# A cross-attention block with its MLP: the same pieces in another written order, score units beside attends

## The chip, the cores and the metric

The kernel runs on one core of a Trainium2 chip. The metric is the device time of one execution in microseconds (us), as a median of several. The core has five engines that run side by side, each through its own instructions in their written order: TensorE (PE, with its weight loads shown apart as PEld), VectorE (DVE), ScalarE (ACT), GpSimd (POOL) and SyncE (SP), which here only issues transfers. They wait for each other through semaphores.

## The reference

Four batches of 512 rows with 512 features, all in float32. Each batch goes through one transformer block with 16 heads of width 32:

```python
x = layer_norm(hidden_states, ln1_w, ln1_b)
q = (x @ q_w + q_b)                          # 16 heads of 32
k = (encoder_hidden_states @ k_w + k_b)
v = (encoder_hidden_states @ v_w + v_b)
scores = einsum("bhqd,bhkd->bhqk", q, k) * scale      # masked
attn = softmax(scores, axis=-1)
out = einsum("bhqk,bhkd->bhqd", attn, v) @ cproj_w + cproj_b
hidden = out + hidden_states
y = layer_norm(hidden, ln2_w, ln2_b)
y = gelu(y @ fc_w + fc_b) @ proj_w + proj_b           # 512 -> 2048 -> 512
return hidden + y
```

## The kernel before

The work is cut into pieces, and a table, `ORDER`, names every step of every piece in the order in which it is written. A loop at the end of the kernel reads the table word by word; each word runs one step of one piece, up to that piece's next `yield`. No scheduler moves anything afterwards: an instruction stands on its engine where its word stands in the table. So the table sets the order on all five engines at once.

The attention is made in 16 windows `w` (batch `w // 4`, a group of four heads `w % 4`). The words that matter here, with the lines of the kernel before:

- `k:w`, `q:w`, `v:w`: the products for K, Q and V of a window on PE (L475, L487, L497), with the copy of the result out of PSUM by ACT. They use the whole 128 x 128 array. A K or Q product is 4 matmuls of 512 columns, a V product 16 of 128 columns. A float32 matmul counts as two instructions in the profile, so these show as x8 and x32.
- `u:w:t`: a score unit (L510), four matmuls, one a head, for 128 query rows `t`. Each uses 32 rows of the array (`32*128` in the profile), the four run at once, and each has its own PSUM bank `sc0` to `sc3`. There is only one set of these four banks.
- `x:w:t`, four words: for each head DVE adds the mask, finds the minimum and moves the scores out of the bank (L518), then ACT takes the exponential (L521).
- `r:w:t`: DVE turns the exponentials in 32 x 32 blocks (L529, L536), two heads at a time; in odd `t` the reciprocal of the row sums (L533) and its own turn (L539) come too.
- `e:w:h` and `d:w:h`: for each half window, twelve transfers of SP and four POOL copies (L546) put the turned blocks where the next product wants them.
- `a:w:h`: an attend, the product of probabilities and V (L568). It uses 32 columns of the array (`128*32`), 16 matmuls, x32 in the profile; DVE then multiplies by the reciprocals (L574).
- `c:b:t`: the output projection (L443); `t1`, `t2` are transposes by PE (L369), `f:b:c` and `P:b:n` the products of the MLP (L621, by a Strassen-like scheme), `fs` the sums of weights that they need (POOL, for most), `j` their joins (ACT copies and DVE additions), `g` the gelu.
- `s1`, `s2`: layer-norm statistics by DVE. `wk`, `wq`, `wv`, `lx`, `lh`, `lf`, `le`: loads that SP issues.

K, Q, V, attends, `c` and the MLP's products take their PSUM result from a ring of four banks.

```python
def scores(w, qt):
    for h in range(HG):
        r = slice(h * HD, (h + 1) * HD)
        nc.tensor.matmul(sc[h], S["qT", w][r, ts(qt, P)], S["kT", w][r, :], start=True, stop=True)
```

Of the kernel before, what the change touches and what calls it, by code (L numbers as in the profile page):

```python
# [77 lines left out]
u:2:3 r:2:1 v:4 x:2:3 x:2:3 k:6 e:1:1 e:1:1 e:1:1 e:2:0 e:2:0 e:2:0 wv:7 d:1:1 na:1 wa:1 na:1 r:2:2 x:2:3 x:2:3 r:2:3
  r:2:3 wa:1 na:1 wa:1 na:1 d:2:0 a:1:1
u:3:0 r:2:2 k:6 wa:1 x:3:0 a:1:1 x:3:0 x:3:0 x:3:0 r:2:3 r:2:3 q:5  # L80
u:3:1 x:3:1 v:5 wv:6 e:2:1 e:2:1 e:2:1 wk:7 wq:7 d:2:0 r:3:0 q:5 x:3:1 x:3:1 x:3:1 v:5 d:2:1 r:3:0 r:3:1 r:3:1 r:3:1
  d:2:1 cb:0 v:3 a:2:0 v:7
u:3:2 q:4 x:3:2 x:3:2 x:3:2 x:3:2 q:4 a:2:0 r:3:1 lf:0:3 e:3:0 e:3:0 e:3:0
u:3:3 a:2:1 q:7 r:3:2 x:3:3 x:3:3 x:3:3 x:3:3
u:4:0 k:7 d:3:0 d:3:0 a:2:1 r:3:2 r:3:3 r:3:3 m:1 r:3:3 r:3:3 x:4:0 x:4:0 x:4:0 x:4:0
u:4:1 r:4:0 v:7 x:4:1 x:4:1 x:4:1 v:6 e:3:1 e:3:1 wv:9 e:3:1 lf:0:2 x:4:1 v:6
u:4:2 r:4:0 r:4:1 a:3:0 x:4:2 x:4:2 k:7 r:4:1 a:3:0 x:4:2 r:4:1 r:4:1 x:4:2 c:0:1 d:3:1 v:4 d:3:1
u:4:3 r:4:2 c:0:0 a:3:1 x:4:3 x:4:3 q:7 x:4:3 c:0:1 r:4:3 x:4:3 c:0:0
u:5:0 r:4:2 r:4:3 x:5:0 x:5:0 a:3:1 x:5:0 x:5:0 c:0:2
u:5:1 c:0:3 s2:0 r:4:3 wk:8 lh:0 d:4:0 cb:0 c:0:2 s2:0 s2:0 r:4:3 le:2 lx:2 le:2 lf:0:1 wq:6 s1:2 wk:9 lh:0 e:4:0  # L90
  e:4:0 e:4:0 le:2 le:2 c:0:0 v:7 fs:0:0 fs:0:0 cb:0 d:4:0 fs:0:1 x:5:1 c:0:3 fs:0:0 m:1 v:6 c:0:1 d:4:1 e:4:1 q:6
  wv:8 e:4:1 e:4:1 d:4:1 x:5:1 r:5:0 x:5:1 x:5:1 a:4:0
u:5:2 v:9 k:8 s2:0 r:5:0 x:5:2 r2:0 r:5:1 n2:0 r:5:1 n2:0 r:5:1 r:5:1 q:6 x:5:2 x:5:2 k:8 x:5:2 c:0:2 c:0:3 n2:0
u:5:3 a:4:0 n2:0 x:5:3 t2:0:1 t2:0:1 r:5:2 t2:0:0 t2:0:0 x:5:3 r:5:2 x:5:3 k:9 a:4:1 x:5:3 r:5:3 v:9 k:9 y:0
u:6:0 x:6:0 d:5:0 fs:0:1 fs:0:1 d:5:0 t2:0:3 t2:0:2 x:6:0 t2:0:2 x:6:0 x:6:0 a:4:1 v:8 f:0:0 t2:0:3 j:0:0 r:5:3 r:5:3
  y:0
u:6:1 y:0 f:0:0 f:0:1 f:0:0 e:5:0 lx:2 wk:10 lx:2 s1:2 lt:2 lt:2 e:5:0 e:5:0 lf:0:3 r:5:3 e:5:1 lx:2 x:6:1 y:0 v:8
  r:6:0 x:6:1 f:0:1 j:0:0 f:0:0 x:6:1 j:0:0 j:0:1 x:6:1 r:6:0
u:6:2 f:0:1 j:0:1 j:0:0 f:0:0 f:0:1 j:0:0 x:6:2 s1:2 r:6:1 r:6:1 j:0:1 f:0:2 fs:0:1 fs:0:2 d:5:1 fs:0:2 s1:2 r1:2
  x:6:2 j:0:1 f:0:1 j:0:1 x:6:2 j:0:0 x:6:2 r:6:1 ts:2 a:5:0 a:5:0 j:0:1 r:6:1  # L100
u:6:3 g:0:0 g:0:0 ts:2 g:0:1 x:6:3 x:6:3 j:0:2 lf:0:4 e:5:1 wk:11 lt:2 lf:0:4 e:5:1 wv:10 wq:8 e:6:0 fs:0:2 d:5:1 k:10
  ts:2 fs:0:2 fs:0:3 lb:2 e:6:0 lb:2 d:6:0 fs:0:3 d:6:0 f:0:2 f:0:2 r:6:2 x:6:3 x:6:3 r:6:2 r:6:3 j:0:2 k:10 r:6:3
  r:6:3
u:7:0 f:0:2 j:0:2 x:7:0 x:7:0 x:7:0 x:7:0 a:5:1
u:7:1 fs:0:4 e:6:0 v:10 wv:11 lf:0:5 a:5:1 r:6:3 e:6:1 lh:1 lf:0:5 x:7:1 v:10 x:7:1 r:7:0 lt:2 fs:0:4 fs:0:3 na:2
  g:0:0 na:2 na:2 fs:0:4 d:6:1 cb:1 a:6:0 x:7:1 x:7:1 wa:2 r:7:0 r:7:1 j:0:2 a:6:0 r:7:1
u:7:2 f:0:4 j:0:4 x:7:2 f:0:4 f:0:4 x:7:2 j:0:4 f:0:2 f:0:4 j:0:2 x:7:2 wa:2 j:0:4 fs:0:4 f:0:3 x:7:2 j:0:4 f:0:4
  r:7:1 e:6:1
u:7:3 na:2 g:0:1 j:0:4 wa:2 wa:2 g:0:4 r:7:1 j:0:4 q:8 q:8 g:0:4 d:6:1 d:7:0 d:7:0 e:6:1 lf:0:6 lf:0:6 fs:0:6 g:0:4
  f:0:3 lh:1 lh:1 e:7:0 e:7:0 e:7:0 x:7:3 x:7:3 r:7:2 x:7:3 x:7:3 a:6:1  # L110
u:8:0 a:6:1 j:0:2 r:7:3 r:7:2 m:2 x:8:0 r:7:3 j:0:3 x:8:0 v:11 x:8:0 x:8:0 r:7:3 a:7:0 wq:9 wq:10 lx:3
u:8:1 f:0:3 r:7:3 a:7:0 j:0:3 v:11 x:8:1 s1:3 e:7:1 fs:0:3 lf:0:7 e:7:1 e:7:1 r:8:0 x:8:1 d:7:1 cb:1 g:0:1 x:8:1 x:8:1
  r:8:1 c:1:1 c:1:1 f:0:3 g:0:2 q:10
# [806 lines left out]
```

## Time and profile before

| | |
|---|---|
| median of 3 runs | 760.53 us (760.25 to 760.59) |
| profiled execution, first to last instruction | 758.0 us |
| DVE busy | 596.2 us (79%) |
| ACT busy | 403.3 us (53%) |
| POOL busy | 371.4 us (49%) |
| DMA, mean share of the 16 DMA engines in use by 40 slices | 0.4 to 0.9 |

The profile names a group of instructions by line, engine and operation, then what it writes and reads (`sc<-pbt` reads `pbt` and writes `sc`), the shape, and how many. In its timeline the first number is the start and the second the duration, in us from the start of the span. Matmuls overlap their neighbours, so the step from one start to the next is the time that a piece costs, and the duration is longer than this step.

### The profile page before, as it was taken

What the parts mean: (1) busy time and instruction counts of PE and PEld (TensorE: products, weight loads), DVE (VectorE), ACT (ScalarE), POOL (GpSimd) and SP (SyncE); (2) the same over time, 40 slices, a digit from 0 to 9 for tenths busy, and PEclk for the clock granted to TensorE, in tenths of its full rate; (3) what the DMA queues carried; (4) which work ended last, traced back from release to release, by engine and by line L of the source; (5) the groups of instructions that cost most, each with busy time, mean ns of one, the idle gap of its engine ahead of it and who ended that gap; (6) DMA issues with size and microseconds to landing.
All of it is one profiled execution on the core that took longest, in us unless ns stands there. A gap on an engine that the chain in (4) does not pass through costs nothing.

```text
span 758.0 us, 14114 instructions
## 1 busy us (share of the span) xinstructions
PE 751.1 (99%) x4925; PEld 534.0 (70%) x4925; DVE 596.2 (79%) x1209; ACT 403.3 (53%) x951; POOL 371.4 (49%) x401
## 2 busy tenths in 40 slices
PE   9999999999999999999999999999999999999998
PEld 6464555467665456665555677766888999999997
DVE  3798999999768888877778986644689799786982
ACT  2566766456777776778867686861343221211110
POOL 1155864743884656656757657854411022240232
PEclk9999999999999999999999999999999999999999
DMA  7698978877887898784977698789545648788575
GB/s 267 199 240 235 251 212 246 232 193 218 212 236 211 229 251 254 204 246 128 248 221 211 209 271 248 219 277 317 163 140 178 247 134 162 225 169 263 99 180 112
DMA packets 72133, 162.18 MB, mean 214 GB/s; under 512 B 11960, under 2 KB 24656, under 8 KB 70400
## 3 DMA queue, kind: packets, MB, share of 16 engines
q1 hardware_dynamic: 56864, 131.44, 59.7%
q0 software_dynamic: 15056, 29.84, 15.9%
q8 instruction: 39, 0.64, 0.4%
q14 instruction: 30, 0.25, 0.1%
q10 hardware_dynamic: 144, 0.02, 0.0%
HBM read 73.95 MB, written 25.18 MB: 131 GB/s over the span
## 4 chain that ended last, share of the span: by engine, by line
PE 96%; DVE 2%; DMA 1%; issue 0%; POOL 0%; ACT 0%; POOLq 0%; DVEq 0%
PE acc L621 37%; PE sc L621 11%; PE sc L510 9%; PE acc L475 8%; PE acc L487 8%; PE acc L443 7%; PE acc L568 7%; PE acc L497 7%; PE acc L369 1%; DMA pbt<-fc_w_dram 1%; PE acc L850 1%; DVE ext L333 0%; DVE swap L330 0%; DVE yT L330 0%; DVE xn L330 0%
## 5 line engine op out<-in xcount | busy, mean ns | idle before, releaser
L521 ACT ACTIVATE ptt<-ptt,mn 128x512 f32<-128x512 f32 x256 | 182.9, 716 | 78.0 <-DVE mn L518 77.5
L518 DVE CUSTOM_DVE_ANT_0 ptt<-sc,mix 128x512 f32<-128x512 f32 x256 | 164.6, 680 | 30.5 <-PE sc L510 29.1
L546 POOL COPY swap<-swap 32x1088 f32<-32x1088 f32 x128 | 139.8, 1092 | 70.0 <-DVE swap L539 43.9
L529 DVE STREAM_TRANSPOSE swap<-ptt 128x1024 f32<-128x1024 f32 x64 | 78.8, 1232 | 9.5 <-DMA pbt<-fc_w_dram 3.2
L536 DVE STREAM_TRANSPOSE swap<-ptt 128x1024 f32<-128x1024 f32 x64 | 78.3, 1224 | 1.8 <-ACT ptt L521 1.8
L510 PE MATMUL sc<-pbt 32*128 32x512 f32 x512 | 73.8, 640 | 0.8 <-ACT pbt L489 0.8
L669 POOL DMA_DIRECT2D gd<-st x32 | 24.4, 766 | 96.9 <-ACT st L667 87.0
L646 ACT COPY st<-acc 128x256 f32<-128x256 f32 x96 | 34.5, 368 | 69.6 <-PE acc L621 66.3
L497 PEld LDWEIGHTS acc<-ptt,ext 128*128 128x128 f32 x512 | 58.7, 192 | 8.7 <-issue 3.4
L621 PE MATMUL acc<-ys,wsum 128*128 128x256 f32 x256 | 64.1, 382 | 0.0
L568 PE MATMUL acc<-swap,mix 128*32 128x256 f32 x1024 | 61.6, 382 | 0.0
L497 PE MATMUL acc<-ptt,ext 128*128 128x128 f32 x512 | 60.8, 277 | 0.0
L646 ACT COPY xn<-acc 128x128 f32<-128x128 f32 x75 | 18.9, 270 | 77.4 <-PE acc L621 72.5
L621 PE MATMUL acc<-yT,pbt 128*128 128x256 f32 x240 | 58.9, 386 | 1.0 <-DVE mix L574 1.0
L475 PE MATMUL acc<-ext,ptt 128*128 128x512 f32 x128 | 59.1, 605 | 0.0
L487 PE MATMUL acc<-ext,ptt 128*128 128x512 f32 x128 | 58.4, 600 | 0.0
L443 PE MATMUL acc<-mix 128*128 128x512 f32 x128 | 58.0, 600 | 0.0
L621 PEld LDWEIGHTS acc<-yT,pbt 128*128 128x128 f32 x240 | 44.0, 190 | 19.7 <-issue 6.9
L621 PEld LDWEIGHTS acc<-ys,wsum 128*128 128x128 f32 x256 | 47.6, 190 | 12.0 <-POOL wsum L330 1.5
L568 PEld LDWEIGHTS acc<-swap,mix 128*32 128x32 f32 x1024 | 30.6, 109 | 31.4 <-issue 9.0
L330 DVE TENSOR_TENSOR st<-acc,st 128x512 f32<-128x512 f32 (+1 forms) x48 | 26.1, 544 | 32.0 <-ACT st L646 22.4
L521 ACT ACTIVATION_READ_ACCUMULATOR ptt<-ptt,mn 128x1 f32 x256 | 48.3, 189 | 0.0
(143 smaller groups left out, 1396.7 us busy)
## 6 DMA issues: line engine op xcount, KB each, us to landing
swap<-swap SPq DMA_DIRECT2D x384, 136.0 KB, 3.4
gd<-st POOLq DMA_DIRECT2D x32, 512.0 KB, 4.7
swap<-gd SPq DMA_DIRECT2D x12, 1024.0 KB, 5.8
pbt<-fc_w_dram SPq DMA_DIRECT2D x40, 256.0 KB, 4.3
xn<-x_dram SPq DMA_DIRECT2D x32, 256.0 KB, 5.3
ext<-fc_w_dram SPq DMA_DIRECT2D x24, 256.0 KB, 2.9
swap<-xn POOLq DMA_DIRECT2D x18, 256.0 KB, 4.7
ptt<-k_w_dram SPq DMA_DIRECT2D x16, 256.0 KB, 4.0
```

The source lines that it names most:

```text
L443: nc.tensor.matmul(acc, oT[:, g, ts(t, P)], wc[:, g, :], start=(g == 0), stop=(g == NG - 1))
L475: nc.tensor.matmul(acc, S["wk", w][:, d, :], eT[:, d, :], start=(d == 0), stop=(d == ND - 1))
L487: nc.tensor.matmul(acc, S["wq", w][:, d, :], xT[:, d, :], start=(d == 0), stop=(d == ND - 1))
L497: nc.tensor.matmul(acc[:, ts(t, P)], eT[:, d, ts(t, P)], S["wv", w][:, d, :], start=(d == 0), stop=(d == ND - 1),)
L510: nc.tensor.matmul(sc[h], S["qT", w][r, ts(qt, P)], S["kT", w][r, :], start=True, stop=True)
L518: nc.vector.tensor_tensor_reduce(out=s, in0=sc[h], in1=mb, scale=1.0, scalar=FMAX, op0=ALU.add, op1=ALU.min, accum_out=mn)
L521: nc.scalar.activation(s, s, AF.Exp, bias=mn, scale=-1.0, accum_out=S["sums", w][:, qt, h : h + 1])
L529: nc.vector.transpose(*two_heads[0])
L536: nc.vector.transpose(*two_heads[1])
L546: nc.gpsimd.tensor_copy(pT[ts(i, HD), i], tb[ts(i, HD), i])
L568: nc.tensor.matmul(av[ts(h, HD), : 2 * P].rearrange(shape, **kw), v[:, t, ts(h, HD)], p[t][h], start=(t == 0), stop=(t == NT - 1),)
L621: nc.tensor.matmul(o, x[:, k], y[:, k], start=(k == 0 and not more), stop=(k == n - 1), skip_group_check=more)
```

## The change

Only the table `ORDER` is written anew. It holds the same words, each as often as before; the functions, tiles and instructions are the same. Because the table is five lines shorter, every line after it has a number smaller by 5 (L510 becomes L505). Two lines of each side:

```diff
-u:2:1 r:1:3 x:2:1 e:1:0 lb:1 e:1:0 lb:1 lt:1 lt:1 lf:0:1 wq:5 wk:6 wv:4 cb:0 d:1:0 v:2 d:1:0 d:1:1 x:2:1 q:3 r:2:0 v:5
...
-u:2:2 r:2:0 x:2:2 x:2:2 x:2:2 x:2:2 r:2:1 r:2:1 a:1:0 v:4
+u:2:1 e:1:1 a:1:0 e:1:1 e:1:1 v:5 x:2:1 x:2:1 k:5 x:2:1 x:2:1
+u:2:2 x:2:2 x:2:2 r:2:1 x:2:2 lt:1 lt:1 x:2:2 v:4 wv:7 na:1 r:2:1 v:4 r:2:1
```

A few counts over the PE order of both programs. Steps between a piece on the whole array and a piece in tiles (score unit or attend), either way: 138 before, 114 now. Score unit and attend next to each other: 25 before, 34 now. Score unit, one attend, score unit, with nothing between: none before, 7 now; two more have only the 8-column transpose of `ts` (L392) beside the attend. Two attends in a row: 2 before, 5 now. On ACT, loads of a function table: 40 before, 34 now.

The first place is on PE, at the second score unit of window 2. Before, a V product and an attend stand between this unit and the next:

```order
L510 MATMUL sc_74<-pbt 128x512
L510 MATMUL sc_75<-pbt 128x512
L510 MATMUL sc_76<-pbt 128x512
L510 MATMUL sc_77<-pbt 128x512
L497 MATMUL acc_79<-ptt,ext 128x128 x16
L568 MATMUL acc_78<-swap,mix 32x256 x16
```

Now the attend alone stands there:

```order
L505 MATMUL sc_74<-pbt 128x512
L505 MATMUL sc_75<-pbt 128x512
L505 MATMUL sc_76<-pbt 128x512
L505 MATMUL sc_77<-pbt 128x512
L563 MATMUL acc_80<-swap,mix 32x256 x16
```

In both the next row writes `sc_74` again. What moved away is the V product, which follows the second unit now.

The second place is on DVE, after the last of the four mask-and-minimum steps of unit 3 of window 0 (`mn_0_3_3`). Before, the turns of the finished unit are spread among the steps of the next one and two statistics:

```order
L536 STREAM_TRANSPOSE swap_104<-ptt_107 128x2x4x4x32
L529 STREAM_TRANSPOSE swap_104<-ptt_107 128x2x4x4x32
L533 RECIPROCAL rsum_0_1_386<-sums_0_220 128x8
L518 ISA ptt_107,mn_1_0_0_398<-sc0_74,mix_103 128x512
L518 ISA mn_1_0_0_398 128x1
L341 BN_STATS st1_1_0_402<-xn4_86 128x6
L342 BN_AGGR mv1_1_401<-st1_1_0_402 128x2
L536 STREAM_TRANSPOSE swap_104<-ptt_107 128x2x4x4x32
L539 STREAM_TRANSPOSE swap_104<-mix_103 128x2x4x32
```

Now all turns stand in one block ahead of the steps of unit 0 of window 1:

```order
L524 STREAM_TRANSPOSE swap_104<-ptt_107 128x2x4x4x32
L531 STREAM_TRANSPOSE swap_104<-ptt_107 128x2x4x4x32
L528 RECIPROCAL rsum_0_1_405<-sums_0_233 128x8
L531 STREAM_TRANSPOSE swap_104<-ptt_107 128x2x4x4x32
L534 STREAM_TRANSPOSE swap_104<-mix_103 128x2x4x32
L513 ISA ptt_107,mn_1_0_0_416<-sc0_74,mix_103 128x512
L513 ISA mn_1_0_0_416 128x1
L513 ISA ptt_107,mn_1_0_1_419<-sc1_75,mix_103 128x512
L513 ISA mn_1_0_1_419 128x1
```

The statistics went to other places. On PE, a K and a V product stood between the units 0 and 1 of window 1; now a K product alone.

The third place is SP, right after the Q weight of window 1 (`wq:1`). Before, the weight of V for window 1 comes next and the Q weight of window 2 is the fourth of these rows:

```order
L327 DMA ptt_107<-v_w_dram 128x512
L327 DMA xn4_86<-x_dram 128x512
L327 DMA pbt_106<-fc_w_dram 128x512 x2
L327 DMA ptt_107<-q_w_dram 128x512
L327 DMA ptt_107<-v_w_dram 128x512
L327 DMA ptt_107<-k_w_dram 128x512 x2
```

Now the load for the residual (`xn4`) and two of the next batch's rows (`xn5`, `xn0`) stand ahead, and the Q weight of window 2 is the tenth of these rows:

```order
L322 DMA xn4_86<-x_dram 128x512
L322 DMA pbt_106<-fc_w_dram 128x512
L322 DMA xn5_87<-x_dram 128x512
L322 DMA ptt_107<-v_w_dram 128x512
L322 DMA xn0_82<-x_dram 128x512
L322 DMA ptt_107<-v_w_dram 128x512
L322 DMA pbt_106<-fc_w_dram 128x512
L322 DMA ptt_107<-k_w_dram 128x512
L322 DMA pbt_106<-fc_w_dram 128x512
L322 DMA ptt_107<-q_w_dram 128x512
```

More of the change, by code (lines that the diff above doesn't have):

```diff
@@ L78 @@
[L78 to L113, printed above, removed]
@@ new lines @@
+u:8:0 m:2 r:7:2 x:8:0 r:7:3 f:0:3 e:7:0 e:7:0 j:0:3 x:8:0 v:11 x:8:0 r:7:3 r:7:3 x:8:0 a:6:1
+u:8:1 x:8:1 x:8:1 f:0:3 j:0:3 wq:10 d:7:0 r:8:0 fs:0:3 q:10 x:8:1 x:8:1 e:7:1 wq:9 j:0:3 f:0:3 j:0:3 d:7:1 g:0:2 g:0:2
+  e:7:1 q:10
+u:8:2 a:7:0 r:8:0 j:0:3 g:0:3 x:8:2 fs:0:5 x:8:2 fs:0:5 r:8:1 x:8:2 r:8:1 f:0:5 r:8:1 e:7:1 a:7:0 c:1:1 c:1:1 d:7:1
+  r:8:2 r:8:1 v:11 q:9 x:8:2
+u:8:3 x:8:3 q:9 x:8:3 wk:11 e:8:0 x:8:3 x:8:3 a:7:1 j:0:5 a:7:1
+u:9:0 r:8:3 k:11 r:8:3 r:8:3 e:8:0 e:8:0 fs:0:5 lx:3 le:3 r:8:3 r:8:2 wq:11 d:8:0 x:9:0 x:9:0 lx:3 d:8:0 le:3 le:3
+  cb:1 x:9:0 x:9:0 r:9:0 r:9:0 c:1:2 f:0:5 f:0:5 c:1:2
```

269 lines of the change are left out of this document (146 added, 123 removed).

## The prediction

> **What bounds the kernel now.** I read the page first, then the busy time by stretches, then PE's waits, then PE's timeline.
>
> ```profile
> span 758.0 us, 14114 instructions
> PE 751.1 (99%) x4925; PEld 534.0 (70%) x4925; DVE 596.2 (79%) x1209; ACT 403.3 (53%) x951; POOL 371.4 (49%) x401
> 20.00:200.00 180.00, 179.18 (x1143) 97.99 (x1146) 165.12 (x366) 116.46 (x290) 100.07 (x102) 1.00 0.82 224
> 200.00:540.00 340.00, 338.86 (x2034) 216.56 (x2027) 249.46 (x533) 236.60 (x506) 222.79 (x250) 1.00 0.80 232
> PE acc L621 <- DVE mix L574: 1.0, 1, 1.0
> PE sc L510 <- ACT pbt L489: 0.8, 1, 0.8
> ```
>
> PE is the bound: 751.1 of 758.0 us, at the full granted clock (1.00). So the order can help in two ways only, by a cheaper sequence of the same products or by fewer waits of PE, and it can hurt by new waits. The stretch 20 to 200 us names the engine that would cause them: DVE is busy 165.12 of 180 us there (92%; the columns of such a row are PE, PEld, DVE, ACT and POOL, each with its count of instructions, then clock, share of the DMA engines and GB/s).
>
> A busy PE may hide waits inside a piece, so I read steps from start to start.
>
> ```profile
> 33.53 3.70 PE L487 MATMUL acc<-ext,ptt 128*128 128x512 f32 x8
> 37.16 1.14 PE L510 MATMUL sc<-pbt 32*128 32x512 f32 x8
> 38.23 3.84 PE L497 MATMUL acc<-ptt,ext 128*128 128x128 f32 x32
> 42.00 1.14 PE L510 MATMUL sc<-pbt 32*128 32x512 f32 x8
> ...
> 77.85 1.93 PE L568 MATMUL acc<-swap,mix 128*32 128x256 f32 x32
> 79.71 1.14 PE L510 MATMUL sc<-pbt 32*128 32x512 f32 x8
> 80.78 3.84 PE L497 MATMUL acc<-ptt,ext 128*128 128x128 f32 x32
> ...
> 432.77 3.60 PE L487 MATMUL acc<-ext,ptt 128*128 128x512 f32 x8
> 436.20 1.03 PE L621 MATMUL acc<-yT,pbt 128*128 128x256 f32 x4
> ...
> 492.06 3.59 PE acc L568 x64
> ```
>
> A Q product between two score units takes 37.16 - 33.53 = 3.63 us, one between two full-array products 436.20 - 432.77 = 3.43. The 0.20 us is what it costs to go from the full array into tiles and back. A score unit takes 1.07 (38.23 - 37.16; 80.78 - 79.71 right behind an attend), an attend 1.86, a V product between units 3.77.
>
> **The change part by part.** (1) *Fewer changes of the array's mode.* The PE order has 138 steps between a full-array piece and a tiled one, and 114 after the change. 24 fewer are 12 returns, at 0.20 us: -2.4 us. PE sets the end, so this counts in full. Three more pairs of attends in a row gain between nothing and 0.14 us each (one pair in this trace takes 3.59 us, against 2 x 1.86); I leave them in the bounds, -2.8 to -2.0.
>
> The Trainium skill, TensorEngine Tiling (Array Packing), section Key Properties, says that changing the tiling mode drains TensorE, not only leaving tiling. By that, a score unit (row tiles) beside an attend (column tiles) would still drain and this term would be nothing. The trace speaks against it: the unit takes 1.07 us behind a K, Q or V product and behind an attend alike.
>
> (2) *Score units too close for their banks.* There is one set of four score banks, so a unit waits until DVE has read the unit before it. How long that takes:
>
> ```profile
> 33.84 0.40 DVE L539 STREAM_TRANSPOSE swap<-mix 128x256 f32<-128x256 f32 x1
> 34.17 0.65 DVE L518 CUSTOM_DVE_ANT_0 ptt<-sc,mix 128x512 f32<-128x512 f32 x1
> ...
> 38.31 0.69 DVE L518 CUSTOM_DVE_ANT_0 ptt<-sc,mix 128x512 f32<-128x512 f32 x1 [0.49 <-PE sc L510]
> ...
> 38.93 0.69 DVE L518 CUSTOM_DVE_ANT_0 ptt<-sc,mix 128x512 f32<-128x512 f32 x1
> ...
> 40.15 0.69 DVE L518 CUSTOM_DVE_ANT_0 ptt<-sc,mix 128x512 f32<-128x512 f32 x1
> ...
> 40.77 1.24 DVE L536 STREAM_TRANSPOSE swap<-ptt 128x1024 f32<-128x1024 f32 x1
> 41.93 1.20 DVE L529 STREAM_TRANSPOSE swap<-ptt 128x1024 f32<-128x1024 f32 x1
> 43.06 0.16 DVE L533 RECIPROCAL rsum<-sums 128x8 f32<-128x8 f32 x1
> ```
>
> The unit starts at 37.16, DVE reads its first bank from 38.31 (1.15 later), one bank each 0.61 us, and the last is read at 40.15 + 0.69 = 40.84, 3.68 us after the unit began. A turn takes a step of 1.16 us, the reciprocal 0.10 (to the next start at 43.16), its own turn 0.33. That a unit really waits on its last bank, PE being in order, shows where this trace has it once:
>
> ```profile
> 197.36 1.14 PE L510 MATMUL sc<-pbt 32*128 32x512 f32 x8
> ...
> 201.36 1.14 PE L510 MATMUL sc<-pbt 32*128 32x512 f32 x8
> ...
> 206.27 1.93 PE L568 MATMUL acc<-swap,mix 128*32 128x256 f32 x32
> 208.13 1.93 PE L510 MATMUL sc<-pbt 32*128 32x512 f32 x8
> 209.99 1.13 PE L621 MATMUL acc<-yT,pbt 128*128 128x256 f32 x4
> ...
> 206.15 1.25 DVE L529 STREAM_TRANSPOSE swap<-ptt 128x1024 f32<-128x1024 f32 x1 [2.22 <-DMA pbt<-fc_w_dram]
> ...
> 208.19 0.69 DVE L518 CUSTOM_DVE_ANT_0 ptt<-sc,mix 128x512 f32<-128x512 f32 x1
> ```
>
> DVE ends the previous unit's last bank at 208.19 + 0.69 = 208.88, and the unit of 208.13 takes 1.86 us (209.99 - 208.13) in place of 1.07: 0.79 us lost, though the row counts as busy.
>
> Now the new order. In the seven places "unit, attend, unit" the second unit would start 1.07 + 1.86 = 2.94 us after the first; its last bank is free 3.68 + 0.06 after it (0.06 from the end of DVE's step to the head's start): 0.76 us lost. In two places a transpose lies beside the attend and 0.4 us are lost. Behind one pair (window 5) and another (window 12) DVE also has a leftover of 0.25 together. Sum: 7 x 0.76 + 2 x 0.41 + 0.25 = 6.4 us. Before, the nearest two units stand 4.0 us apart (197.36 and 201.36).
>
> Elsewhere it is a run of units that outpaces DVE. Wait = DVE's work since it last waited for a unit + 1.22 (1.15 + 0.06 and rounding) - PE's distance. First case, from unit 3 of window 0 to unit 1 of window 1, the second place of the order: PE has a V and a K product between, 1.07 + 3.77 + 1.07 + 3.63 = 9.54 us; DVE has 8 banks x 0.61 + 3 turns x 1.16 + 0.10 + 0.34 for the row sums = 8.80. Wait: 8.80 + 1.22 - 9.54 = 0.5. The same sum gives 0.7 more up to unit 0 of window 2 (seven units stand 4.7 to 5.0 us apart there, and each unit brings DVE 2.44 + 2.32 us of banks and turns before anything else), 1.0 in windows 2 and 3, 1.1 in windows 4 and 5: 3.3 in all. For the order before, the same sum finds no wait. Together 6.4 + 3.3 = +9.7 us. Bounds: +6.4, where the turns go beside other work; +14.2, where I put durations (1.24, 0.69) in place of steps. I take 9.7, since the steps are what DVE showed back to back. A PE that waits here gives the time back nowhere: all its products stand behind, in order.
>
> (3) *What was lost before.* The wait at 208 (0.79) and the idle 1.0 for DVE's mix right behind it come of one late load (2.22 on `pbt` above); the order there is new, so I take them as gone, -1.8; bounds 0 and -2.8 (all that PE lacks between 20 and 540 us, 0.82 + 1.14, and that 0.79).
>
> (4) *Weight sums nearer to their products.* POOL makes the sums that an MLP product reads.
>
> ```profile
> L333 POOL TENSOR_TENSOR wsum<-pbt,wsum 128x256 f32<-128x256 f32 x20 | 14.8, 746 | 3.0 <-PE acc L621 2.4
> L546 POOL COPY swap<-swap 32x1088 f32<-32x1088 f32 x128 | 139.8, 1092 | 70.0 <-DVE swap L539 43.9 <-DVE mix L574 13.4 <-PE sc L510 8.0
> swap<-swap SPq DMA_DIRECT2D x384, 136.0 KB, 3.4
> ptt<-q_w_dram SPq DMA_DIRECT2D x16, 256.0 KB, 4.2
> 22.17 0.33 SPq L327 DMA_DIRECT2D ptt<-q_w_dram  x1
> 28.69 3.50 PE L497 MATMUL acc<-ptt,ext 128*128 128x128 f32 x29
> L667 ACT ACT_TABLE_LOAD x20 | 25.7, 1283 | 0.3
> ```
>
> Of 32 MLP pieces, 10 have a third sum with less than 1.8 us of PE work between its word and its product; 4 before. Each of the six more can cost a sum of 0.75 us: between 0 and +4.5; I take +1.0, near the low end, because PE's delays of (2) give POOL time.
>
> (5) *At no cost.* The first loads: window 2's Q weight stands behind five more loads, but it waits for its buffer until the first Q product ends (22.17) in both orders. Its product now stands in the place of the V product of 28.69, so 4.2 us to landing leave about 2; without that cover it costs as much as the load is late, 1 to 2 us. Transfers and copies between turn and attend: twelve transfers, issued over 7 us, and 3.4 to landing, beside 4 x 1.09 on POOL, so 10.5 us; the nearest attend in the new order stands 12.5 us behind its turn. Six loads of function tables fewer take 6 x 1.28 us from ACT, which is 53% busy and ends no large wait of PE.
>
> **Sum.** 758.0 - 2.4 + 9.7 - 1.8 + 1.0 = 764.5 us for the profiled execution. The median is 760.53 - 758.0 = 2.5 us longer than that span, so 767.0 us.
>
> **The rivals.** *No change.* Only the pairs wait (+6.4), all old waits go (-2.8), the modes give -2.8: +0.8, 761.3 us. For it: DVE is idle 15 us between 20 and 200, so its turns may fit. Against it: that idle time stands elsewhere than the runs of units.
>
> *Faster.* DVE starts on a unit as soon as its first head is done. In a pair the second unit's heads start apart, as at 208; if DVE's first bank came 0.8 us earlier than 1.15 behind the start, pair waits vanish and the rest shrinks to nothing: 758.0 - 2.4 - 1.8 + 1.0 + 2.5 = 757.3. It decides where 1.15 becomes 0.4. Against it: unit after unit in this trace shows 1.15 or more.
>
> *POOL is late.* All six sums of (4): 767.0 + 3.5 = 770.5. For it: POOL issues transfers too and waits in order; against it: POOL is 49% busy.
>
> *The change doesn't save what it says.* An attend beside a unit drains as well, by a mechanism that the rows above do not show: 767.0 + 2.4 = 769.4 us. That is the quoted rule of the Trainium skill's tiling page.
>
> **How the numbers follow.** 0.66 for the forecast (its own range 763 to 771: 6.4 to 9.7 and some for the waits, 0 to 2.8 for the old ones), 0.12 for no change, 0.08 for faster, 0.10 for late sums, 0.04 for no saving. A measurement of this kernel tells 0.2% (1.5 us) from no change. Faster: 0.08. The no-change rival lies within, with a part of it above: 0.10. Slower: 0.82. The range reaches from the no-change case to the late sums with part of the upper bound of (2): 760.0 to 773.0 us; it leaves out the faster case and the far ends, some 0.15.
>
> **What would show it.** In the profile after: a second unit in each of the seven pairs with a step of about 1.83 us in place of 1.07; a first long unit at window 1, unit 1; Q products next to full-array ones at 3.43 more often; PE's wait list still short, since waits hide inside units. Wrong would be units at 1.07 everywhere (then DVE keeps pace), or PE idle for transfers, POOL sums or first loads, which I hold for small.

## The result, and the profile after

The changed kernel takes 773.85 us (median of 4 runs, 773.17 to 775.47) against 760.39 us (4 runs, 759.61 to 760.59) before. The ratio is 1.0183, 95% interval 1.0168 to 1.0197: slower by 13.5 us. The prediction said 767.0 us and a range of 760 to 773: the side is right, the size is not.

The page of the changed kernel:

```profile
span 771.1 us, 14133 instructions
PE 760.0 (99%) x4925; PEld 543.5 (70%) x4925; DVE 608.8 (79%) x1209; ACT 397.8 (52%) x945; POOL 374.6 (49%) x401
L505 PE MATMUL sc<-pbt 32*128 32x512 f32 x512 | 85.2, 640 | 1.1 <-ACT pbt L484 1.1
```

The score units' row before:

```profile
L510 PE MATMUL sc<-pbt 32*128 32x512 f32 x512 | 73.8, 640 | 0.8 <-ACT pbt L489 0.8
```

The changed kernel's busy time by stretches, in the columns of the prediction's rows:

```profile
20.00:200.00 180.00, 179.22 (x1110) 99.53 (x1109) 161.44 (x356) 111.73 (x279) 100.64 (x101) 1.00 0.81 224
200.00:540.00 340.00, 338.82 (x2025) 216.22 (x2024) 261.57 (x539) 231.84 (x509) 218.42 (x241) 1.00 0.79 228
540.00:771.00 231.00, 223.45 (x1707) 214.53 (x1705) 178.04 (x297) 49.58 (x154) 53.61 (x52) 0.99 0.64 168
```

And PE's longest waits (engine and line, what it waited for, us in total, times, longest):

```profile
PE acc L364 <- DVE xn L357: 2.2, 1, 2.2
PE acc L616 <- ACT xn L641: 2.0, 1, 2.0
PE acc L845 <- POOL nhalf L834: 1.3, 1, 1.3
PE sc L505 <- ACT pbt L484: 1.1, 2, 0.8
```

Line numbers are 5 lower than before. PE is again busy to 99%, and it is "busy" 8.9 us longer with the same 4925 matmuls: the score units alone (L505) rose from 73.8 to 85.2 us. From 20 to 540 us PE idles as long as before, 1.96 us (0.78 + 1.18); behind 540 us it lacks 7.6 us (231.00 - 223.45), where before it lacked 3.6. The row of before:

```profile
540.00:758.00 218.00, 214.41 (x1673) 206.16 (x1671) 174.56 (x295) 46.15 (x151) 45.74 (x42) 1.00 0.66 174
```

Since waits hide in busy time, I took each PE piece's step from start to start and subtracted what it takes where nothing waits: 1.07 us a unit, 1.86 an attend, 0.112, 0.216 and 0.429 a matmul of 128, 256 and 512 columns, and 0.20 a return between the full array and tiles. What is left over, in us:

| | before | changed | difference |
|---|---|---|---|
| ahead of the first unit | 3.80 | 2.84 | -0.96 |
| score units | 0.78 | 12.55 | +11.77 |
| other pieces up to the last attend | 2.20 | 1.51 | -0.69 |
| everything behind the last attend | 1.29 | 7.05 | +5.76 |
| changes of mode | 13.59 | 11.23 | -2.36 |
| the steps themselves (attends in a row are shorter) | | | -0.41 |

The sum is +13.1 us, the difference of the two spans (771.1 - 758.0). The row of the mode changes is their number at a fixed price, a count and not a measurement of its own. The price is the same in both traces: a stretch on the full array between two tiled pieces takes 0.197 us more than its bare steps before and 0.194 now (medians of 68 and 56 stretches).

So there are two losses: the units, and a stretch behind the last attend for which the prediction has no term.

The units first, in PE's timeline of the changed kernel (start, us, engine, line):

```profile
76.65 1.14 PE L505 MATMUL sc<-pbt 32*128 32x512 f32 x8
77.72 1.93 PE L563 MATMUL acc<-swap,mix 128*32 128x256 f32 x32
79.59 1.93 PE L505 MATMUL sc<-pbt 32*128 32x512 f32 x8
81.45 0.82 PE L492 MATMUL acc<-ptt,ext 128*128 128x128 f32 x5
...
114.58 1.24 DVE L524 STREAM_TRANSPOSE swap<-ptt 128x1024 f32<-128x1024 f32 x1
115.30 1.14 PE L505 MATMUL sc<-pbt 32*128 32x512 f32 x8
117.39 0.84 DVE L452 TENSOR_SCALAR mix<-m 128x512 f32<-128x512 uint8 x1
118.38 0.69 DVE L513 CUSTOM_DVE_ANT_0 ptt<-sc,mix 128x512 f32<-128x512 f32 x1
120.00 2.42 PE L505 MATMUL sc<-pbt 32*128 32x512 f32 x8
122.35 0.82 PE L492 MATMUL acc<-ptt,ext 128*128 128x128 f32 x5
```

u:2:2, behind u:2:1 and one attend, steps 1.86 us (81.45 - 79.59): 0.79 lost, as at 208 us before. The unit of 120.00 stands a whole K product behind the last one and still steps 2.35 us: DVE read the first bank of the unit of 115.30 (u:4:0) only at 118.38, 3.1 us behind its start, since turns and a mask tile came first.

Then the stretch behind 540 us:

```profile
543.63 1.82 DVE L357 TENSOR_SCALAR xn<-xn,mv,rs 128x512 f32<-128x512 f32 x2 [1.21 <-POOL rs L352]
545.38 1.21 DVE L328 TENSOR_TENSOR mix<-pbt 128x512 f32<-128x512 f32 x1
546.51 2.22 DVE L325 TENSOR_TENSOR ext<-swap 128x512 f32<-128x512 f32 x1
547.31 0.38 PE L364 MATMUL acc<-ident,xn 128*128 128x128 f32 x2
548.65 1.59 DVE L357 TENSOR_SCALAR xn<-xn,mv,rs 128x512 f32<-128x512 f32 x2
549.85 0.89 PE L364 MATMUL acc<-ident,xn 128*128 128x128 f32 x3 [2.15 <-DVE xn L357]
```

DVE normalises two row tiles of the last batch, then makes two sums (words pt:7 and xs:0:4) that PE does not need yet, then the other two row tiles. PE's next piece is the turn of these tiles, and it waits 2.15 us. Before, the turns stand in one piece:

```profile
539.97 1.91 PE L369 MATMUL acc<-ident,xn 128*128 128x128 f32 x16
```

Right behind this wait the granted clock falls (the third number from the end of a row):

```profile
552.00:554.00 2.00, 2.00 (x9) 1.73 (x8) 2.00 (x4) 0.78 (x2) 0.00 (x0) 0.50 0.00 0
```

It is 0.50 for 3.4 us, from 550.8 us on. PE works there at half speed, which no list of waits shows; by an estimate from these two figures it loses 1.7 us. Of the 5.76 us, 4.0 are then more idle time (7.55 - 3.59) and 1.7 the slower clock.

### The profile page after: what moved, and what is told of

It is laid out like the page before. It is cut to its first block, busy times and chain, and to the rows that moved or that the text cites. A ratio compares the mean times of both kernels' runs of the same rounds, so it can differ in the third digit from the quotient of the medians.

```text
span 771.1 us, 14133 instructions
## 1 busy us (share of the span) xinstructions
PE 760.0 (99%) x4925; PEld 543.5 (70%) x4925; DVE 608.8 (79%) x1209; ACT 397.8 (52%) x945; POOL 374.6 (49%) x401
## 4 chain that ended last, share of the span: by engine, by line
PE 92%; DVE 2%; DMA 2%; POOL 1%; ACT 1%; issue 1%; DVEq 0%; POOLq 0%; ACTq 0%
PE acc L616 35%; PE sc L616 10%; PE sc L505 10%; PE acc L492 8%; PE acc L438 7%; PE acc L563 7%; PE acc L470 7%; PE acc L482 6%; DMA swap<-xn 2%; PE acc L364 1%; PE acc L845 0%; DMA xn<-x_dram 0%; DVE ptt L513 0%; DVE ext L325 0%; POOL ext L328 0%
## 5 line engine op out<-in xcount | busy, mean ns | idle before, releaser
L541 POOL COPY swap<-swap 32x1088 f32<-32x1088 f32 x128 | 141.4, 1104 | 65.0 <-DVE swap L531 24.2
L505 PE MATMUL sc<-pbt 32*128 32x512 f32 x512 | 85.2, 640 | 1.1 <-ACT pbt L484 1.1
L664 POOL DMA_DIRECT2D gd<-st x32 | 23.9, 749 | 85.2 <-ACT st L641 32.5
L563 PEld LDWEIGHTS acc<-swap,mix 128*32 128x32 f32 x1024 | 30.5, 109 | 35.3 <-issue 10.3
L505 PEld LDWEIGHTS sc<-pbt 32*128 32x128 f32 x512 | 27.2, 182 | 32.9 <-DVE mn L513 13.0
```

The source lines that it names most:

```text
L541: nc.gpsimd.tensor_copy(pT[ts(i, HD), i], tb[ts(i, HD), i])
L563: nc.tensor.matmul(av[ts(h, HD), : 2 * P].rearrange(shape, **kw), v[:, t, ts(h, HD)], p[t][h], start=(t == 0), stop=(t == NT - 1),)
```

## The experiments

In a_n2_late, b_pairs and b_doubles some products or sums read an operand before its new contents are written, so their numbers differ; the instructions are the same. Spans are of one profiled execution, ratios are to the kernel before.

### The stretch behind the last attend

**a_tail_b and b_tail_a** exchange the last words (behind u:15:3) between the two orders.

> The changed order up to and with u:15:3, then all remaining words in the order of before. Theory (the changed kernel's 5.9 us of PE waits after 540 us come from how the last words are ordered): 5 to 6 us less than the changed kernel, about 768 us, ratio to before about 1.0105, and PE's waits on DVE's xn (L357) and ACT's xn (L641) gone. Rival (they are inherited from the attention stage, where DVE and POOL fell behind): no gain, 773 to 774 us, ratio about 1.018.

> The order of before up to and with u:15:3, then all remaining words in the order of the change. Theory (the order of the last words alone costs 5.9 us): 5 to 6 us more than before, about 766 us, ratio about 1.0075. Rival (the late stretch is only slow because of what came ahead of it): 760 to 761 us, ratio 1.000.

a_tail_b: 770.42 us, 1.0138 (1.0122 to 1.0153). b_tail_a: 765.43 us, 1.0071 (1.0045 to 1.0096). With before's last words the excess behind the last attend is 1.29 us, with the changed ones 7.04 behind the order of before: it goes with the words alone. The slower clock is not needed for it: in b_tail_a's profiled execution the clock is 1.00 from 525 to 550 us and 1.000 in the mean of the span. Behind the last attend PE is idle 0.9 us longer there than in the changed kernel, and from that attend to the end both take 239.7 us. PE's waits in b_tail_a show the two of the changed kernel:

```profile
PE acc L616 <- ACT xn L641: 2.4, 1, 2.4
PE acc L364 <- DVE xn L357: 2.2, 1, 2.2
```

a_tail_b gained 3.4 us and not 5 to 6, because where the two orders meet (an attend at 502 us) PE waits for something new:

```profile
PE acc L563 <- ACT st L646: 2.6, 1, 2.6
```

**a_n2_first** moves the two sums of the timeline above.

```diff
-n2:3 n2:3 pt:7 xs:0:4 n2:3 n2:3 t2:3:1 fs:3:0 pt:4 ps:6 fs:3:1 pt:3 t2:3:0 t2:3:0
+n2:3 n2:3 n2:3 n2:3 t2:3:1 fs:3:0 pt:4 ps:6 fs:3:1 pt:3 pt:7 xs:0:4 t2:3:0 t2:3:0
```

> The changed order with two words moved: pt:7 and xs:0:4, written between the second and the third step of the last batch's normalisation n2:3, now stand behind its fourth step and ahead of the second turn t2:3:0. Theory (DVE does 3.4 us of sums ahead of the rows that PE must turn): the 2.2 us wait of PE on DVE's xn at 549.9 us goes, 2.2 to 4.3 us less than the changed kernel, 770 to 771.5 us, ratio 1.013 to 1.0155. Rival (the wait was for something else that is late, or the sums are then late for the next product): within 0.5 us of the changed kernel, ratio 1.018.

774.93 us, 1.0196 (1.0172 to 1.0220): no gain. The wait on the normalisation is gone (the turns at 548.43 take 2.06 us in one piece), and another stands right behind:

```profile
548.43 2.06 PE L364 MATMUL acc<-ident,xn 128*128 128x128 f32 x16
```

Among PE's waits of the same kernel:

```profile
PE acc L616 <- DVE yT L372: 2.5, 1, 2.5
```

The turned tiles are evicted by DVE too (yT, L372), and the sums now stand ahead of that.

**a_n2_late and a_n2_late2** were to move all five sums behind the chain.

> The changed order with five words moved: the first pt:7, xs:0:4, pt:4, ps:6 and pt:3 behind the last batch's n2:3, sums on DVE of 0.7 to 1.2 us an instruction, now stand one by one among the joins behind y:3, not ahead of or between the normalisation, the turns and the y sums. Theory (in this stretch the chain norm, turn, y sums, first product runs over DVE, and every sum written into it is paid by PE): the excess of the turns, 3.6 us, and of the products behind them, 0.8 us, goes: 3.5 to 4.4 us less than the changed kernel, about 769.8 us, ratio about 1.013, and the wait on ACT's xn (L641, 2.0 us at 660 us) stays. Rival (DVE has more work up to there than time, in any order): PE waits as long at a later product, ratio 1.017 to 1.020.

> The changed order with five words moved: pt:7 and xs:0:4, written between the second and the third step of the last batch's normalisation n2:3, and pt:4, ps:6 and pt:3, written between its steps and the turns, now stand one by one among the joins behind the y sums y:3. Theory (in this stretch the chain norm, turn, y sums, first product runs over DVE, and every sum written into it is paid by PE; moved only behind the norm, they were paid at the turn's eviction): the turns' excess of 3.6 us and the 0.8 us behind them go, 3.5 to 4.4 us less than the changed kernel, about 769.8 us, ratio about 1.013. Rival (DVE has more to do up to there than there is time for, in any order): PE waits as long at a later product, ratio 1.017 to 1.020.

In a_n2_late the words moved are the next ones of the same names, and the two between the steps of the normalisation stand where they were: the 2.2 us wait stayed, 775.36 us, 1.0201 (1.0186 to 1.0216). a_n2_late2 moves the first ones:

```diff
-n2:3 n2:3 pt:7 xs:0:4 n2:3 n2:3 t2:3:1 fs:3:0 pt:4 ps:6 fs:3:1 pt:3 t2:3:0 t2:3:0
+n2:3 n2:3 n2:3 n2:3 t2:3:1 fs:3:0 fs:3:1 t2:3:0 t2:3:0
...
+y:3 y:3 y:3 pt:5 j:3:0 f:3:1 j:3:1 pt:7 f:3:1 f:3:1
```

771.11 us, 1.0142 (1.0128 to 1.0156), some 3 us less than the changed kernel. The turns' excess falls from 3.58 to 0.26 us. But the products behind 608 us lose 1.95 us more (4.49 in place of 2.54). The second wait is only 0.3 us longer (2.3 in place of 2.0); the rest is the clock, which now falls to 0.50 behind this wait, again for 3.4 us:

```profile
PE acc L616 <- ACT xn L641: 2.3, 1, 2.3
658.00:660.00 2.00, 2.00 (x11) 2.00 (x11) 0.00 (x0) 0.99 (x3) 0.46 (x1) 0.50 1.14 261
```

**a_tail_fix** tried that one.

```diff
-P:1:1 pj:1:1 la:1:7 pj:0:7 pt:7 P:0:7 pj:0:7 P:0:3 pt:1 P:1:1 gs:1:5 P:1:1 P:1:4 gs:1:6 pj:1:1 J:0:4 J:0:6 pj:0:5 J:0:5
+la:1:7 pj:0:7 pt:7 P:0:7 pj:0:7 P:0:3 pt:1 gs:1:5 gs:1:6 J:0:4 J:0:6 pj:0:5 J:0:5 P:1:1 pj:1:1 P:1:1 P:1:1 P:1:4 pj:1:1
```

> The changed order with the five sums behind the y sums (as a_n2_late2) and, besides, the words of batch 1's first two projections that stood ahead of J:0:4, J:0:6 and J:0:5 (P:1:1 three times, pj:1:1 twice, P:1:4) moved behind J:0:5, where the order of before has them. Theory (ACT's copy into xn waits for a row that a transfer still reads, because the next batch's projection is begun before the joins of this one): the wait of 2.3 us on ACT's xn at 657 us goes, and most of the 4.5 us of excess in the products behind 608 us: 2 to 4 us less than a_n2_late2, 767 to 769 us, ratio 1.009 to 1.0115. Rival (the wait is for another row or transfer): 771 us, ratio 1.014.

770.79 us, 1.0144 (1.0129 to 1.0159): the wait is still there (2.6 us), so the rival holds. So it is not these words that take the row too early. In the changed kernel's timeline ACT stands 6.5 us for a transfer that reads xn; which word makes that transfer late stays open.

```profile
660.18 0.27 ACT L641 COPY xn<-acc 128x128 f32<-128x128 f32 x1 [6.51 <-DMA swap<-xn]
```

### Whether the early lateness makes the later one

**b_then_a6** takes before's words up to u:6:0 and the change's from there.

> The order of before up to u:6:0, then all remaining words in the order of the change (124 changes of tile mode). Theory (each stretch's waits belong to its own order): of the changed kernel's excess over before this keeps the score units' waits behind 172 us, 6.5 us, and the 5.9 us behind 540 us, and saves 7 returns, 1.4 us, and 0.5 us of older waits: 10 to 10.5 us more than before, about 770.5 us, ratio 1.0135. Rival (the lateness of DVE in windows 0 to 5 is carried on and makes the later waits): the later score waits shrink to what before has, 0.8 us, and the ratio is 1.006 or less.

776.86 us, 1.0219 (1.0205 to 1.0233). The units' excess is 6.76 us, as forecast, though windows 0 to 5 ran like before, and the stretch behind the last attend is 7.50. So each stretch's waits come from its own words; the rival falls. The total is 6 us above the forecast. At the place where the orders meet PE waits 3.4 us, and the clock is 0.50 for 6.8 us, which by an estimate is up to 3.4 us more:

```profile
PE acc L616 <- DVE st L325: 4.5, 3, 3.4
```

### What a pair of units costs

**a_no_pairs and a_no_pairs2** break eight of the nine pairs by a full-array product between. The second of the eight:

```diff
-u:6:2 x:6:2 x:6:2 a:5:0 ts:2 ts:2 x:6:2 x:6:2 u:6:3 j:0:1 r:6:1 x:6:3 x:6:3 k:10
+u:6:2 x:6:2 x:6:2 a:5:0 ts:2 ts:2 x:6:2 x:6:2 k:10 u:6:3 j:0:1 r:6:1 x:6:3 x:6:3
```

> The changed order with eight of its nine 'unit, attend, unit' pairs broken up: for each, the next full-array product that was written behind the second unit is written ahead of it (c:0:3, k:10, f:0:4 with its two sums, k:11, t2:1:0, f:1:1, f:1:3, c:2:3); the pair of u:2:1 and u:2:2 stays. It has 128 changes of tile mode in place of 114, 7 returns more. Theory (the second unit waits for DVE to leave the score banks): the eight waits in the changed kernel's trace add up to 5.7 us and go; the mode changes cost 7 x 0.20 = 1.4 us; so 4.3 us less than the changed kernel, about 769.5 us, ratio to before about 1.0125. Rival (DVE is simply behind there, and PE will wait for it at the next unit whatever stands between): the waits come back within one or two units and the time is 774 to 775 us, ratio 1.018 to 1.020.

> The changed order with the same eight pairs broken up again, now only by products that have nothing to wait for: c:0:3, k:10, k:11, k:13 and k:14 go ahead of the second unit, and v:10, f:1:4 and c:2:2, written ahead of the first unit, go behind the attend. 128 changes of tile mode, 7 returns more than the changed kernel. Theory (the second unit of a pair waits for DVE to leave the banks, and only there): the eight waits of 5.7 us go, 7 x 0.20 = 1.4 us of mode changes come, 4.3 us less than the changed kernel, about 769.5 us, ratio to before about 1.0125. Rival (DVE or the ring of accumulators is behind there anyway): new waits stand at other pieces of the same windows and the ratio is 1.017 or more.

Both are slower than the change: 778.76 us, 1.0241 (1.0224 to 1.0258), and 780.82 us, 1.0275 (1.0250 to 1.0300). The units' excess falls from 12.55 to 7.77 and 8.60 us, by 4.8 and 4.0 of the 5.7 that were forecast, and the seven returns count for 1.38. But the other pieces' excess rises from 1.51 to 8.36 and 11.36 (by an estimate 1.4 and 1.7 of it come of a clock of 0.50 from 205.7 and 205.6 us on). The largest new wait of both:

```profile
PE acc L616 <- ACT st L641: 3.3, 1, 3.3
```

k:10 stood between u:6:3 and the products f:0:2, and covered ACT's copies out of the accumulators that f:0:2 needs. Moved ahead of the unit, it uncovers them. Both times are above what either forecast of a_no_pairs gives; the rival of a_no_pairs2 (new waits at other pieces) is right. This product was not only a gap between two units, it also covered something.

**b_pairs_min** goes the other way: six pairs in the order of before, by six products moved and nothing else, q:7 for instance. **b_pairs** had tried nine, with the loads and sums beside them moved too: 789.82 us, 1.0392 (1.0375 to 1.0410), with new waits of up to 4.6 us for POOL's sums; it tells little of the pairs.

```diff
-u:3:3 a:2:1 q:7 r:3:2 x:3:3 x:3:3 x:3:3 x:3:3 u:4:0 k:7
+u:3:3 a:2:1 r:3:2 x:3:3 x:3:3 x:3:3 x:3:3 u:4:0 q:7 k:7
```

> The order of before with nine 'unit, full-array product, attend, unit' (or attend first) made into 'unit, attend, unit' and the product behind: at u:2:1, u:2:3, u:3:1, u:3:3, u:4:3, u:7:0, u:7:1, u:8:0 and u:9:3. 120 changes of tile mode in place of 138. Nothing else of the change. Theory: nine second units wait 0.79 us each, 7.1 us, and nine returns less save 1.8 us: 5.3 us more than before, about 765.5 us, ratio 1.007; in the trace the second units step in 1.86 us in place of 1.07. Rival (a pair costs nothing by itself, the units of the changed kernel wait since DVE was behind there for other reasons): 1.8 us less than before, ratio 0.9976.

> The order of before with six full-array products alone moved, so that six 'unit, attend, unit' pairs arise: v:5 behind u:2:2, k:6 behind u:3:0, q:7 behind u:4:0, c:0:0 behind u:5:0, v:11 behind u:8:1, q:11 behind u:9:3. 126 changes of tile mode in place of 138; every other word where it was. Theory: six second units wait 0.79 us each, 4.7 us, six returns less save 1.2 us: 3.5 us more than before, about 763.7 us, ratio 1.0046. First rival (DVE is nearly full in windows 2 to 6, and a unit that is pulled ahead of a 3.5 us product is late by most of that): 1.2 to 2.5 us a pair in the first four, ratio 1.007 to 1.012. Second rival (a pair costs nothing by itself): ratio 0.9984.

b_pairs_min: 775.48 us, 1.0221 (1.0183 to 1.0258), above both forecasts: the first rival's direction, at a higher price. Six returns less count for 1.18 us. The second units lose 10.3 us: 2.76 (u:2:2), 2.18 (u:3:0), 0.79 (u:4:0), 2.53 (u:5:0), 0.44 (u:8:1), 1.61 (u:9:3). Besides, two attends that now come earlier wait 3.5 us for their operands. The longer of these waits (2.9 us) stands between u:8:0 and u:8:1, so DVE had time to read the banks; the 0.44 us of u:8:1 is the clock, 0.57 in the mean from 242 to 246 us. A dear pair and the cheap one, in the timeline:

```profile
74.98 0.69 DVE L513 CUSTOM_DVE_ANT_0 ptt<-sc,mix 128x512 f32<-128x512 f32 x1
75.60 1.24 DVE L524 STREAM_TRANSPOSE swap<-ptt 128x1024 f32<-128x1024 f32 x1
76.73 2.15 PE L505 MATMUL sc<-pbt 32*128 32x512 f32 x6
77.01 0.69 DVE L513 CUSTOM_DVE_ANT_0 ptt<-sc,mix 128x512 f32<-128x512 f32 x1 [0.17 <-DVE swap L524]
77.63 1.24 DVE L524 STREAM_TRANSPOSE swap<-ptt 128x1024 f32<-128x1024 f32 x1
78.79 0.65 DVE L513 CUSTOM_DVE_ANT_0 ptt<-sc,mix 128x512 f32<-128x512 f32 x1
80.56 1.61 PE L492 MATMUL acc<-ptt,ext 128*128 128x128 f32 x12
...
112.56 1.14 PE L505 MATMUL sc<-pbt 32*128 32x512 f32 x8
112.59 1.20 DVE L524 STREAM_TRANSPOSE swap<-ptt 128x1024 f32<-128x1024 f32 x1
113.72 0.69 DVE L513 CUSTOM_DVE_ANT_0 ptt<-sc,mix 128x512 f32<-128x512 f32 x1
115.50 1.93 PE L505 MATMUL sc<-pbt 32*128 32x512 f32 x8
```

Around 75 us two turns stand between the reads of u:2:1's banks, and u:2:2 behind it takes 3.83 us (80.56 - 76.73) in place of 1.07. At 112.59 a turn runs while PE still writes u:3:3; then the banks are read back to back, and u:4:0 loses 0.79. So the distance on PE is one part of the price, and DVE's words between are the other.

**b_pairs_x** keeps the six pairs and moves those words: x words ahead, turns behind.

```diff
-u:3:3 a:2:1 r:3:2 x:3:3 x:3:3 x:3:3 x:3:3 u:4:0
+u:3:3 x:3:3 x:3:3 a:2:1 r:3:2 x:3:3 x:3:3 u:4:0
```

> The order of before with the six pairs of b_pairs_min, and in these six units alone the x words (DVE reads the score banks) moved ahead of the turns and other words, as far as the six score tiles let them: one or two turns of 1.24 us go from ahead of the last x word to behind it at u:2:1, u:4:3, u:8:0 and u:9:2; at u:2:3 the tiles allow no change of weight. Theory (a pair waits for the DVE words between, not for the distance alone): 1.2 us less at three of them, 2.5 us less at u:8:0, about 6 us less than b_pairs_min, 769.5 us, ratio to before about 1.0125. Rival (what is put behind is missed at once, as with all x words moved): 775 us or more, ratio 1.02 or above.

779.65 us, 1.0251 (1.0224 to 1.0278): the rival, no gain over b_pairs_min. u:2:2 gained 0.7 us, but the cheap pair became dear (2.32 us lost in place of 0.79):

```profile
114.05 0.69 DVE L513 CUSTOM_DVE_ANT_0 ptt<-sc,mix 128x512 f32<-128x512 f32 x1 [1.16 <-PE sc L505]
...
115.28 1.24 DVE L524 STREAM_TRANSPOSE swap<-ptt 128x1024 f32<-128x1024 f32 x1
115.72 1.13 PE L505 MATMUL sc<-pbt 32*128 32x512 f32 x4
116.69 0.69 DVE L513 CUSTOM_DVE_ANT_0 ptt<-sc,mix 128x512 f32<-128x512 f32 x1 [0.17 <-DVE swap L524]
```

The x word is now first, finds the unit not yet written, and DVE idles 1.16 us; the turn that had filled this time stands between the banks. The units' excess is only 0.9 us above b_pairs_min's; of the 3.1 us by which the profiled execution is longer, about half (by an estimate 1.7 us) is one more stretch of 3.4 us with the clock at 0.50.

**a_x_first, b_x_first and a_all_fix** do that everywhere: every x word as early as the six score tiles allow, in both orders, and together with a_tail_fix. In the changed order for instance:

```diff
-u:3:2 r:3:1 a:2:0 r:3:0 a:2:1 lx:2 r:3:1 x:3:2 x:3:2 x:3:2 x:3:2 a:2:0 d:3:0 r:3:2 u:3:3
+u:3:2 r:3:1 a:2:0 r:3:0 x:3:2 x:3:2 x:3:2 x:3:2 a:2:1 lx:2 r:3:1 a:2:0 d:3:0 r:3:2 u:3:3
```

> The changed order with only the x words moved: each of the four words in which DVE reads a score bank (and ACT takes the exponential) stands as early behind its unit as the six score tiles allow, ahead of turns, sums and evictions. TensorE's order and its 114 changes of tile mode are those of the change. Theory (a unit waits for the DVE words that are written ahead of the x words of the unit before it; where nothing stands between, a pair still waits 0.79 us): of the 11.8 us of score waits above before's, the nine pairs' 6.7 us stay and about 5 us go: 769 us, ratio to before about 1.0115. Rival (DVE is nearly full in windows 2 to 6, and what is put behind is missed as soon): waits at attends and at products for evictions take their place, ratio 1.017 or more.

> The order of before with the x words moved in the same way. Theory: before has 0.8 us of score waits and 1.3 us at the product behind one of them to win, and DVE's words are in step with TensorE there: 758.5 to 761 us, ratio 0.998 to 1.001. Rival (what is put behind the x words, turns and evictions, is missed): slower by 3 us or more, ratio above 1.004, with new waits at attends or products.

> a_x_first and a_tail_fix together. Theory (the two losses are separate): the gains add up, 7 to 9 us less than the changed kernel, 764 to 766.5 us, ratio 1.005 to 1.008. Rival (TensorE that comes earlier waits elsewhere): the later of the two gains is given back, ratio 1.010 or more.

848.56 us, 1.1182 (1.1147 to 1.1217); 836.23 us, 1.1001 (1.0985 to 1.1018); 843.82 us, 1.1111 (1.1064 to 1.1158). DVE's waits, in a_x_first and then in the changed kernel:

```profile
DVE ptt L513 <- PE sc L505: 94.1, 42, 8.0
```

```profile
DVE ptt L513 <- PE sc L505: 36.8, 31, 6.2
```

DVE works in order. A word that stands early stops all words behind it until PE has written its bank, up to 8.0 us, and PE then lacks the evictions and sums behind. Part of the price is the clock: its mean falls to 0.980, 0.981 and 0.984 (0.998 in the changed kernel), by an estimate 17, 16 and 14 us of the three spans.

**b_doubles** wanted the mode changes without pairs, by two attends between two units, window 2 for instance:

```diff
-v:3 a:2:0 v:7 u:3:2 q:4 x:3:2 x:3:2 x:3:2 x:3:2 q:4 a:2:0 r:3:1 lf:0:3 e:3:0 e:3:0 e:3:0 u:3:3 a:2:1 q:7 r:3:2
+v:3 v:7 u:3:2 q:4 x:3:2 x:3:2 x:3:2 x:3:2 q:4 r:3:1 lf:0:3 e:3:0 e:3:0 e:3:0 u:3:3 a:2:0 a:2:1 r:3:2
```

> The order of before with the two attends of a window put side by side between two units, 'unit, attend, attend, unit', in eleven windows (0, 1, 2, 4, 5, 7, 8, 10, 11, 12, 13), the full-array products between them written behind the second unit. 114 changes of tile mode, as many as the changed kernel, but no two units closer than two attends (3.7 us). Theory (mode changes cost 0.20 us a return, and units wait only when DVE has not had the time): 12 x 0.20 = 2.4 us less than before and no bank waits, about 758 us, ratio 0.997. Rival (any order with so few mode changes bunches DVE's, ACT's or the accumulators' work, and gives the saving back): 761 to 765 us, ratio 1.001 to 1.006, with waits at the moved products or attends.

897.03 us, 1.179 (1.1733 to 1.1847). The loads and evictions that moved along came too late (attends waited up to 13.9 us for transfers), and the mean granted clock is 0.935, by an estimate 58 of the 896 us; of two attends between units by themselves it tells nothing.

### First loads, and a better order

**a_open_b** takes the change's words ahead of u:0:0 and before's from there.

> The opening words of the change (all ahead of u:0:0: first loads, first products, first normalisation) and then all remaining words in the order of before. Theory from the changed kernel's trace, where the first unit starts 1.0 us earlier: 0.9 us less than before, about 759.3 us, ratio 0.9988. Rival (the transfers that the new opening pushes back are missed in windows 0 and 1): no gain, ratio 1.000 or above.

759.62 us, 0.9993 (0.9985 to 1.0002): no gain. The 0.96 us that the table gives to the opening is not the opening's: with before's opening words the same excess was 3.80 in one kernel, 2.85 in b_tail_a and 4.18 in b_doubles.

**b_best** moves three words in the order of before; the eviction:

```diff
-cb:1 a:6:0 x:7:1 x:7:1 wa:2 r:7:0 r:7:1 j:0:2 a:6:0 r:7:1 u:7:2
+cb:1 a:6:0 x:7:1 x:7:1 a:6:0 wa:2 r:7:0 r:7:1 j:0:2 r:7:1 u:7:2
```

> The order of before with three words moved: the eviction of a:6:0 (DVE, mix<-acc, 0.41 us) from behind two turns and a sum to directly behind the last x:7:1, a:9:1 to behind the turn of the statistics so that it stands beside u:11:0, and f:2:0 from ahead of u:14:3 to ahead of a:13:0 so that this attend stands beside the unit: 134 changes of tile mode in place of 138. Theory: the product behind u:7:2 no longer waits 1.0 us for the accumulator that a:6:0 holds, and two returns less save 0.4 us: 1.4 us less than before, about 759 us, ratio 0.9982. Rival (every word that leaves its place is missed somewhere): ratio 1.000 to 1.003.

760.12 us, 0.9997 (0.9984 to 1.0009): no difference. At the product behind u:7:2 the excess fell from 1.28 to 0.42 us, and two returns less count for 0.40. But both moves for the mode changes met a wait of 0.8 us, a:9:1 for an accumulator that ACT had still to empty, and f:2:0, now earlier, for its turned operand:

```profile
PE acc L563 <- ACT yT L374: 0.8, 1, 0.8
...
PE acc L616 <- DVE yT L372: 0.8, 1, 0.8
```

The eviction alone was not tried. No order here beats the one before.

## Why the prediction was right and wrong

The sum for the profiled execution was 764.5 us; it took 771.1. The 6.6 us come out of its own steps:

- **(1) Mode changes, -2.4:** right. Twelve stretches on the full array between tiled pieces fell away, at 0.20 us each: -2.36. The price is the same where such stretches were added or removed by hand (medians of 0.197 in a_no_pairs and 0.196 in b_pairs_min). The three more attends in a row gave 0.41, inside the bounds.
- **A reading in (1) that is wrong:** the prediction takes a unit's 1.07 us as a sign that going from attend to unit costs nothing. In the changed kernel an attend takes 1.86 us ahead of a unit as ahead of a product, and 1.75 ahead of another attend. So leaving an attend for a unit costs 0.11 us, as much as leaving it for a product; it stands at the end of the attend, where the unit's step can't show it. The Trainium skill (TensorEngine Tiling (Array Packing), Key Properties) says that a change of tiling mode drains TensorE. This trace agrees with it between attend and unit (1.86 against 1.75 us). The term would not be nothing by that rule: with the 25 and 34 contacts of unit and attend, the changes of mode are 163 before and 148 now, 15 fewer, which are the twelve stretches and the three attends in a row.
- **(2) Units too close, +9.7:** measured 12.55. The pairs were sized right: 6.4 predicted, 6.5 measured. Six of the seven bare pairs lose 0.79 to 0.93 us (the prediction's own terms, 3.68 + 0.06 - 2.94, give 0.80 and not the 0.76 written there); u:9:0 loses 0.39, since its attend had waited. The two with a transpose lose 0.59 in place of 0.41. Mis-sized were the runs of units that outpace DVE: 3.3 predicted, 6.0 measured. Of this 1.7 lie behind 200 us (windows 7, 8, 10 and 14), where the sum had found none. In windows 1 to 5 the sum was too small by about 1.0: up to u:2:0 1.4 for 1.2, in windows 2 and 3 1.2 for 1.0, in 4 and 5 1.7 for 1.1. At u:4:0 DVE began 3.1 us behind the unit's first matmul, where 1.15 is its least, since it was still at turns and a mask tile written ahead; which words the sum left out there is not on record.
- **(3) Old waits gone, -1.8:** the wait at 208 us is gone (0.78), the other pieces gained 0.69; -1.5.
- **(4) POOL's sums, +1.0:** PE waited for none of them.
- **(5) Opening, transfers, function tables at no cost:** holds.
- **The step that failed** is one that is missing. The part-by-part sum ends with the last attend, and says nothing of the last batch's MLP and the projections, though the diff writes those words anew too: +5.76 us. "PE idle for transfers, POOL sums or first loads, which I hold for small" did hold for what PE itself waits for; PE idled for DVE's normalisation and ACT's copies (one of them late for a transfer), which were not on that list, and behind the first of these waits the granted clock, which the prediction takes as 1.00, was 0.50 for 3.4 us. Shown by b_tail_a, where these words alone cost about 5 us (1.0071). What makes that transfer late stays open.

With that term the sum would have been off by 0.8 us. The 2.85 us of (2) are balanced by the 1.0 of (4), by the opening's 0.96, which is chance, and by 0.4 of attends; (3) fell 0.3 short.

The rivals: "no change" and "faster" fall with the units' waits; "POOL is late" and "no saving" fall with (4) and (1), although "POOL is late", at 770.5 us, came nearest to the time, for a wrong reason.

## What to carry to other kernels

In an order that keeps PE busy to 99% and DVE nearly full in stretches, a piece is also the cover for what stands behind it: price a move by what it uncovers as well as by what it saves, and price every stretch that the diff writes anew, the last one too, where nothing stands behind to cover a wait. The reader of a buffer belongs neither late nor as early as possible in an engine's queue, but where its operand is just ready; here a ready word ahead of it was free, and a waiting one stopped all others. A return of 0.2 us saved did not pay for a unit that stands too close (0.8 us). After a long wait, look at the granted clock as well as at the list of waits.

## What was not expected

- Of six pairs made in the same way, five cost their second units 0.8 to 2.8 us, by what DVE does between them; what made one of them cheap was a turn ahead of the first read.
- Moving only the x words (DVE's reads and ACT's exponentials), with TensorE's order untouched, cost 75 us in the changed order and 76 in the order of before.
- The time ahead of the first unit varies by over 1 us from one execution to another with the same words (excess 2.83 to 4.18 us), more than the gain that one execution of the change seemed to show.
- The granted clock fell to 0.50 for 3.4 us, or a multiple of it, after PE had lost 2.4 us or more within 7 us, but not each time: b_tail_a waits 2.2 and 2.4 us and its mean stays at 1.000. By an estimate such a stretch costs PE up to half its length; behind the last attend the two kernels took as long with it as without.
